# Moving the next image's first score unit out of the MLP's first block to the end of the clustering, with projection fillers kept for behind the group norm

## The chip, the cores and the metric

The kernel runs on one core of a Trainium2 chip. The metric is the device time of one execution in microseconds (us), taken as the median of several runs. All data are 32-bit floats. The engines of a core are called PE (matrix), DVE (vector), ACT (scalar), POOL (GpSimd) and SP (which here only issues DMA transfers).

## The reference

The input is four images of 256 channels and 64 x 64 pixels. Each goes through two layers:

```
# layer 0: self-attention over the 4096 pixels
q = wq x + bq (32 channels);  k = wk x + bk (32);  v = wv x + bv (256)
x = gamma * (v softmax(q^T k)^T) + x
# layer 1
y = x + ls1 * cluster(group_norm(x))     # four-centre clustering in four heads
h = w2 gelu(w1 group_norm(y) + b1) + b2  # 256 -> 1024 -> 256, per pixel
y = y + ls2 * h
z = relu(batch_norm(y * dw_w));  out = relu(batch_norm(pw_w z))
```

Both group norms take one mean and one variance over all channels and pixels of an image.

## The kernel before, in words

The images are worked one after the other, but overlapped. For each image `b` the main loop runs three stages in program order: `weighting` (softmax and weighted sum of the attention, in 8 pixel blocks of 8 units each), `cluster`, and `mlp` (8 blocks of 512 pixels; in the last image but one, 7). The order of instructions on each engine is the order written in the program; a framework adds the semaphores and hands out the buffers.

PE work of the next image is put into the current image's stages in two ways.

- **Fillers.** `parts.projections` is a list of 35 small pieces of the next image's projections: 32 halves of `v` (`v_half`, line 314, four rows of the trace's PE pieces each, and an ACT copy, line 322, after every second one), and, from place 26 on, `k_half(0)` (line 291), `q_four(0)` (line 333, its ACT step is line 341) and `k_half(1)`. `fill(n)` takes the next `n` of the list. They are called wherever PE would wait for another engine: in the weighting's end, in the clustering and in the group norms. `fill(N)` takes all that is left.
- **Score units.** `score(u)` computes a unit of the next image's attention scores: four matmuls (line 363) of 32 rows each, which need the query block in the layout that `q_block` makes with four DMA transfers (line 348). Given the list arguments it copies the two score banks to SBUF with ACT (lines 371 and 372), and appends to the list `maxima` the DVE steps (line 376) that take the running maximum: two of them for unit 0, four for the others. `rest()` takes one step from that list, before and after the third and fourth chunk of each block of the MLP.

In `mlp`, `at` says after which chunk of which block a unit stands. A block has four chunks `j`; each chunk is `first(nb, j)`, seven products of 256 columns (line 1361, tiles hp, hq and hr) and their sums on DVE (line 1352), with the second layer's seven steps (line 1278, tile mo) of the chunk before put between them. `slots` says how many of these seven go to each of four places, and it differs for a chunk that a score unit follows:

```python
                    todo = second_by_seven(nb, acc, hs, j, own, ahead)
                    slots = (0, 2, 2, 3)
                    if scored:
                        slots = (3, 1, 2, 1)
                    elif j == 2 and nb:
                        slots = (3, 1, 0, 3)
```

`norm(nb)` writes the normalised block and its factors, the sums and differences that the seven products need (lines 1239 to 1242). Block 0 has them from DVE, with the scaling (line 1176); later blocks have the factors from POOL, within the third chunk's second-layer steps, which run during the fourth chunk's products.

At the end of the clustering the result is added to the image (`products`, PE line 982, DVE line 994, ACT line 1006 with POOL line 1007), and DVE gathers the second group norm's statistics (line 966). `mlp` then starts with POOL's weight factors (lines 1157, 1158, 1159 and 1162) and `group_norm`: statistics to one mean per partition (DVE, line 243), across partitions (PE, lines 245 and 246, tile gnm), DVE lines 249, 250 and 253, PE line 255 (tile gnv), then the root (DVE 171, ACT 172, DVE 174) and scale and shift (DVE 263 and 264). One filler stands after line 246 and one after the root.

Buffers that matter: the two score banks in PSUM (`ps_s`, two buffers) also serve the products hp, hq and hr and the clustering's `products`; projections use `ps_m` (two); a score's result is one of 14 `spool` tiles; the running maximum is a single buffer.

Of the kernel before, what the change touches and what calls it, by code (L numbers as in the profile page):

```python
# [14 lines left out]
B, C, H, W = 4, 256, 64, 64  # L15
# [3 lines left out]
NBLK = N // NB  # L19
# [26 lines left out]
def attention_then_cluster_block(  # L46
# [17 lines left out]
    nc = tc.nc  # L64
# [22 lines left out]
    def load_x(b, t):  # L87
        xb = x[b].rearrange("(k p) h w -> p k (h w)", p=P)
        xt = spool.tile([P, KC, XT], F32, tag="s", name=f"x_{b}_{t}")
        for k in range(KC):  # L90
            nc.sync.dma_start(out=xt[:, k, :], in_=xb[:, k, t * XT : (t + 1) * XT])
        return xt
# [597 lines left out]

    h64_q = h64[:ED].rearrange("p (q h m) -> p q h m", q=4, h=HEADS)

    def cluster(b, ys, stats, cells, rest, fill, gelu):

        pool = small.tile([P, KC, 4, 4], F32, tag="pool", bufs=1, name=f"pool_{b}")

# [264 lines left out]
        stats2 = small.tile([P, 2 * NBLK, 6], F32, tag="stats", name=f"st2_{b}")  # L961
        pieces = {}

        def seen(hb, c):
            for q in range(4):
                nc.vector.bn_stats(stats2[:, 4 * q + 2 * hb + c, :], pieces[hb, c, q])
# [54 lines left out]
        seen(0, 1)  # L1021
        seen(1, 0)
        seen(1, 1)
        fill(5)
        return stats2


# [104 lines left out]
    def turn_w2(b, kept):  # L1132


        a11, _, a21, a22 = quarters_w2()
        w7 = work.tile([P, h_n, P], F32, tag="rden", bufs=1, name=f"w2_7_{b}")
        nc.gpsimd.tensor_tensor(w7, a21, a11, ALU.subtract)
        s1 = work.tile([P, h_n, P], F32, tag="q", name=f"w2_1_{b}") if kept else a21
        nc.gpsimd.tensor_tensor(s1, a21, a22, ALU.subtract)
        s2 = work.tile([P, h_n, P], F32, tag="q", name=f"w2_2_{b}")  # L1140
        nc.gpsimd.tensor_tensor(s2, s1, a11, ALU.subtract)
        return s1, s2, w7

    def mlp(b, ys, stats2, fill, nxt, blocks, turned):


        W_A, W_CD, W_B, W_D = own_w["q"]
# [101 lines left out]

        for _ in norm(0, nc.vector):  # L1250
            pass
        if nxt:
            nxt.q_block(0, nc.sync)

        def product(out, w, j, x):
            nc.tensor.matmul(out, w[:, j * P : (j + 1) * P], x, start=True, stop=True)
# [179 lines left out]

        hooks, drips, maxima = [], [], []

        def hook():
            while hooks:
# [6 lines left out]
        acc, todo, slots = None, iter(()), (0,) * 4  # L1449
        own = ahead = iter(())  # L1450

        at = {(u, 3): u for u in range(7)} | {(7, 2): 7}
        if blocks < NBLK:
            at |= {(6, 1): 6, (6, 2): 7}
            del at[6, 3]
        for nb in range(blocks):
            end = nb == blocks - 1
            for j in range(4):
# [37 lines left out]
                if scored:  # L1496
                    copies = []
# [37 lines left out]
    def filler(todo):  # L1535
        def fill(n):
            for _ in range(min(n, len(todo))):
                todo.pop(0)()

        return fill  # L1540

    with tc.manual_schedule():
        here = attention(0, xs0)
        here.alone()
        late = None
        for b in range(B):
            xs1, begun = [], []
            nxt = attention(b + 1, xs1) if b + 1 < B else None

            def ahead():  # L1550
                if nxt and len(xs1) < N // XT:
                    xs1.append(load_x(b + 1, len(xs1)))
                elif late and not begun:
                    begun.append(begin())

            begin, todo, gelu = late or (None, list(nxt.projections) if nxt else [], lambda i: None)
            fill = filler(todo)
            stats, cells, rest = here.weighting(ahead, fill, (lambda: None) if b else derived)
            turned = turn_w2(b, not nxt)
            stats2 = cluster(b, here.xs, stats, cells, rest, fill, gelu)  # L1560

            late = mlp(b, here.xs, stats2, fill, nxt, NBLK - (b == B - 2), turned)
            here = nxt


# [74 lines left out]
```

## Time and profile before

| what | us |
|---|---|
| median of 3 runs (lowest to highest) | 3378.88 (3378.66 to 3379.28) |
| the profiled execution's own time | 3378.26 |
| its span, first to last instruction | 3376.5 |
| PE busy | 3318.5 |
| DVE busy | 2226.3 |
| POOL busy | 1929.7 |
| ACT busy | 1687.1 |

The busy times of different engines overlap, so they don't add up to the span. A row of the timeline gives the start, the duration of a run of equal instructions, the engine, the line, and in brackets how long the engine had been idle and which engine ended that. PE matmuls overlap with their successors by design; the distance between starts is what one costs.

### The profile page before, as it was taken

Reading aid. Unit: us, or ns where it says so; the run is one execution under the profiler, and the core shown is the slowest. Engines: PE = TensorE matmul, PEld = TensorE weight load, DVE = VectorE, ACT = ScalarE, POOL = GpSimd, SP = SyncE. Lnnn points to the kernel's source line nnn. Section 1 sums busy time; section 2 is a strip of 40 time slices with the busy share of each in tenths; the row PEclk is TensorE's granted clock in tenths of the full one; section 3 lists DMA queues with packets and bytes.
Section 4 is the critical chain, followed back from the end, with each engine's and each line's share of the span. In section 5 each row is a group of like instructions: output and inputs, shape, how many; then the busy total and the mean of one; then the engine's idle time right before and its main releaser. Section 6 shows DMA issues by size and latency. Waiting matters only on the chain.

```text
span 3376.5 us, 34772 instructions
## 1 busy us (share of the span) xinstructions
PE 3318.5 (98%) x12322; PEld 1815.5 (54%) x12322; DVE 2226.3 (66%) x3546; ACT 1687.1 (50%) x2253; POOL 1929.7 (57%) x1366
## 2 busy tenths in 40 slices
PE   8999999999999999999999999999999999999999
PEld 4434445788533444578843334457873344346686
DVE  5667664677666766467766676646766766764675
ACT  5545543445555554345555555434555555544444
POOL 2655666366365666536645566554644676573664
PEclk9999999999999999999999999999999999999999
DMA  2000002000000000100000000020000000010000
GB/s 71 13 13 11 16 7 86 4 13 19 25 13 13 13 13 22 70 4 19 14 29 13 10 13 13 22 71 4 20 26 13 13 13 13 10 39 1 13 20 26
DMA packets 43102, 70.99 MB, mean 21 GB/s; under 512 B 9680, under 2 KB 18480, under 8 KB 42928
## 3 DMA queue, kind: packets, MB, share of 16 engines
q1 hardware_dynamic: 38064, 61.94, 5.5%
q10 hardware_dynamic: 4608, 6.30, 0.8%
q8 instruction: 97, 1.59, 0.2%
q14 instruction: 77, 0.63, 0.1%
q0 software_dynamic: 256, 0.52, 0.1%
HBM read 43.46 MB, written 16.89 MB: 18 GB/s over the span
## 4 chain that ended last, share of the span: by engine, by line
PE 94%; DVE 4%; ACT 1%; POOL 0%; issue 0%; DMA 0%; SPq 0%; ACTq 0%; POOLq 0%; DVEq 0%
PE av L477 53%; PE mo L1278 10%; PE sc L363 8%; PE hq L1361 5%; PE hp L1361 3%; PE hr L1361 3%; PE vp L314 2%; PE fv L861 2%; PE mo L1262 1%; PE hq_pw L1361 1%; PE pw L1215 1%; PE hr_pw L1361 1%; PE op L982 1%; PE hp_pw L1361 1%; PE qp L333 0%; PE kp L291 0%
## 5 line engine op out<-in xcount | busy, mean ns | idle before, releaser
L477 PE MATMUL av<-s,v 128*128 128x512 f32 x4096 | 1819.2, 598 | 0.6 <-ACT s L467 0.6
L472 POOL TENSOR_TENSOR acc<-acc,s 128x1024 f32<-128x1024 f32 x448 | 1057.1, 2360 | 538.3 <-ACT s L467 519.5
L477 PEld LDWEIGHTS av<-s,v 128*128 128x128 f32 x4096 | 759.0, 190 | 1044.8 <-issue 1034.5
L467 ACT ACTIVATE s<-s 128x1024 f32<-128x1024 f32 x512 | 541.0, 1059 | 591.1 <-DVE s L464 550.2
L464 DVE TENSOR_TENSOR s<-s,mb 128x1024 f32<-128x1024 f32 x512 | 595.8, 1206 | 18.4 <-ACT mb L448 16.7
L385 DVE TENSOR_TENSOR top<-sc,top 128x1024 f32<-128x1024 f32 x196 | 239.4, 1222 | 374.7 <-PE sc L363 374.6
L1316 ACT ACTIVATE hs<-hs,pv_s 128x256 f32<-128x256 f32 x496 | 233.3, 505 | 339.2 <-DVE hs L1352 339.2
L1278 PE MATMUL mo<-hs,w 128*128 128x256 f32 x1512 | 387.9, 382 | 0.0
L381 ACT COPY s<-sc 128x1024 f32<-128x1024 f32 x224 | 225.1, 1005 | 225.6 <-PE sc L363 225.6
L1278 PEld LDWEIGHTS mo<-hs,w 128*128 128x128 f32 x1512 | 282.0, 190 | 60.2 <-ACT hs L1316 19.9
L363 PE MATMUL sc<-q,k 32*128 32x512 f32 x2048 | 299.9, 640 | 0.4 <-ACT s L386 0.4
L388 DVE TENSOR_TENSOR top<-sc,top 128x1024 f32<-128x1024 f32 x196 | 240.1, 1225 | 72.6 <-ACT s L381 59.6
L386 ACT COPY s<-sc 128x1024 f32<-128x1024 f32 x224 | 227.3, 1015 | 66.0 <-DVE top L383 36.1
L1352 DVE TENSOR_TENSOR hs<-hq,hs 128x256 f32<-128x256 f32 x496 | 198.5, 421 | 75.5 <-PE hq L1361 65.2
L469 POOL TENSOR_TENSOR acc<-s 128x1024 f32<-128x1024 f32 x32 | 75.3, 2352 | 287.6 <-ACT s L467 287.6
L1285 POOL TENSOR_TENSOR hs<-hs 128x256 f32<-128x256 f32 x108 | 82.3, 762 | 194.5 <-ACT hs L1369 91.4
L363 PEld LDWEIGHTS sc<-q,k 32*128 32x128 f32 x2048 | 86.4, 182 | 183.1 <-issue 122.0
L1352 DVE TENSOR_TENSOR hs<-hp,hs 128x256 f32<-128x256 f32 x124 | 52.1, 420 | 143.0 <-ACT hs L1369 143.0
L1361 PE MATMUL hr<-xn,w 128*128 128x256 f32 x496 | 127.5, 379 | 0.5 <-DVE hs L1352 0.5
L314 PE MATMUL vp<-wv_s,x 128*128 128x256 f32 x512 | 123.4, 387 | 0.2 <-ACT v L322 0.2
L314 PEld LDWEIGHTS vp<-wv_s,x 128*128 128x128 f32 x512 | 93.5, 190 | 25.5 <-issue 10.5
L1361 PEld LDWEIGHTS hr<-xn,w 128*128 128x128 f32 x496 | 94.1, 190 | 19.1 <-issue 4.8
(261 smaller groups left out, 3528.0 us busy)
## 6 DMA issues: line engine op xcount, KB each, us to landing
x<-in_x SPq DMA_DIRECT2D x32, 512.0 KB, 6.7
out<-xn SPq DMA_DIRECT2D x62, 256.0 KB, 2.1
w<-in_w SPq DMA_DIRECT2D x8, 1024.0 KB, 10.7
mr<-row_mx SPq DMA_DIRECT2D x28, 256.0 KB, 3.1
rden<-row_rd SPq DMA_DIRECT2D x28, 256.0 KB, 3.1
q<-q ACTq DMA_DIRECT2D x96, 64.0 KB, 2.0
mix<-in_wfv SPq DMA_DIRECT2D x8, 192.0 KB, 8.4
q<-q SPq DMA_DIRECT2D x24, 64.0 KB, 2.1
```

Source lines behind the costliest of these rows:

```text
L314: nc.tensor.matmul(vps[0][:, i % 2, :], xs[i * P // XT][:, k, o : o + P], wv_s[:, k, :], start=(k == 0), stop=(k == KC - 1),)
L363: nc.tensor.matmul(halves[r // 2][:, r % 2, :], k_s[rows, g, :], q_s[rows, :], start=True, stop=True)
L385: nc.vector.tensor_tensor(top, halves[1], top, ALU.max)
L388: nc.vector.tensor_tensor(top, halves[0], top, ALU.max)
L464: nc.vector.tensor_tensor(sh, sh, mxs[nb].unsqueeze(1).to_broadcast([P, 2, NB]), ALU.subtract)
L467: nc.scalar.activation(sh, sh, AF.Exp)
L472: nc.gpsimd.tensor_tensor(acc, acc, s[:, 2 * h : 2 * h + 2], ALU.add)
L477: nc.tensor.matmul(av[c], own["v"][:, RG * g + quarter, c * P : (c + 1) * P], slots[u][:, quarter, :], start=(g == 0 and quarter == 0), st ...
L1278: return nc.tensor.matmul(bank[:, half * HB : (half + 1) * HB], a[:, j], t, start=start, stop=stop)
L1316: nc.scalar.activation(src, src, AF.Gelu_apprx_tanh, bias=pvc("b1", P, j + 4 * (i > 1)))
L1352: nc.vector.tensor_tensor(dst, ps, term, ALU.add)
L1361: nc.tensor.matmul(out, w, x, start=True, stop=True)
```

## The change

For an image that has a next one, the end of `cluster` no longer takes five fillers. It issues `q_block(0)` of the next image, takes three fillers, and computes score unit 0 with both its copies. The two fillers not taken there remain in the list for `group_norm` and `fill(N)` in `mlp`. In `mlp` the issue of `q_block(0)` and the place of unit 0 after block 0's fourth chunk go away, and with it the slots of a scored chunk there. The list `maxima` is made in the main loop and passed on, so unit 0's two maximum steps are taken in block 0 instead of block 1.

```diff
-    def cluster(b, ys, stats, cells, rest, fill, gelu):
+    def cluster(b, ys, stats, cells, rest, fill, gelu, nxt, maxima):
...
         seen(1, 1)
-        fill(5)
+        if not nxt:
+            fill(5)
+            return stats2
+
+        nxt.q_block(0, nc.sync)
+        fill(3)
+        copies = []
+        nxt.score(0, copies, maxima)
+        copies.pop()()
         return stats2
...
-    def mlp(b, ys, stats2, fill, nxt, blocks, turned):
+    def mlp(b, ys, stats2, fill, nxt, blocks, turned, maxima):
...
         for _ in norm(0, nc.vector):
             pass
-        if nxt:
-            nxt.q_block(0, nc.sync)
...
-        hooks, drips, maxima = [], [], []
+        hooks, drips = [], []
...
-        at = {(u, 3): u for u in range(7)} | {(7, 2): 7}
+        at = {(u, 3): u for u in range(1, 7)} | {(7, 2): 7}
...
-            stats2 = cluster(b, here.xs, stats, cells, rest, fill, gelu)
-
-            late = mlp(b, here.xs, stats2, fill, nxt, NBLK - (b == B - 2), turned)
+            maxima = []
+            stats2 = cluster(b, here.xs, stats, cells, rest, fill, gelu, nxt, maxima)
+
+            late = mlp(b, here.xs, stats2, fill, nxt, NBLK - (b == B - 2), turned, maxima)
```

Line numbers behind the change move by up to 8 in the changed kernel (line 1361 becomes 1367, line 1352 becomes 1358, line 1240 becomes 1248).

## The prediction

> **What bounds the kernel now.** I read three views of the profile, from coarse to fine. First the page: busy times, and the chain that ended last.
>
> ```profile
> PE 3318.5 (98%) x12322; PEld 1815.5 (54%) x12322; DVE 2226.3 (66%) x3546; ACT 1687.1 (50%) x2253; POOL 1929.7 (57%) x1366
> ...
> PE 94%; DVE 4%; ACT 1%; POOL 0%; issue 0%; DMA 0%; SPq 0%; ACTq 0%; POOLq 0%; DVEq 0%
> ```
>
> The matrix engine (PE) is the bound: 3376.5 of span less 3318.5 leaves 58 us of idle in all. A change can win only by putting work into these gaps. So the second view is who PE waited for (us in total, times, longest):
>
> ```profile
> PE hp L1361 <- DVE xn L1240: 4.0, 4, 1.7
> ...
> PE hp L1361 <- DVE hs L1352: 3.6, 4, 0.9
> ...
> PE hp L1361 <- DVE xn L1176: 2.4, 3, 0.8
> ...
> PE gnv_gn L255 <- DVE mv_gn L250: 1.7, 4, 0.4
> ```
>
> These four are in one place, the second group norm and the MLP's first products, once per image; for each of images 0 to 2 the waits in that place are 0.4, 0.8, 0.8 and 0.9 us. The third view is the timeline there, for image 0 (images 1 and 2 repeat it to 0.03 us, 838.52 and 1675.09 us later).
>
> ```profile
> 645.60 2.49 SPq L348 DMA_DIRECT2D q<-q  x4
> ...
> 647.67 3.72 PE L314 MATMUL vp<-wv_s,x 128*128 128x256 f32 x16
> ...
> 650.30 0.59 DVE L243 BATCH_NORM_AGGREGATE mv_gn<-st 128x2 f32<-128x96 f32 x1
> ...
> 651.22 0.28 PE L245 MATMUL gnm_gn<-mv_gn,left 128*128 128x1 f32 x2
> ...
> 651.76 1.27 POOL L1159 TENSOR_TENSOR w_bcd<-w,w_abcd 128x512 f32<-128x512 f32 x1
> 651.96 1.09 DVE L250 SCALAR_TENSOR_TENSOR mv_gn<-dv_gn,mv_gn 128x1 f32<-128x1 f32 x1
> ...
> 653.10 0.38 PE L255 MATMUL gnv_gn<-mv_gn,avg 128*128 128x1 f32 x2 [0.40 <-DVE dv_gn L253]
> ...
> 655.27 0.70 PE L1361 MATMUL hp<-xn,w 128*128 128x256 f32 x2 [0.81 <-DVE xn L1176]
> ...
> 656.74 0.67 PE L1361 MATMUL hp<-xn,w_abcd 128*128 128x256 f32 x2 [0.77 <-DVE xn L1240]
> ```
>
> The reader is to see that a serial VectorE (DVE) chain runs from 650.30 to 656.60 and that PE, with its fillers, is early three times. Every f32 matmul prints as two pieces, so vp x16 is eight matmuls, four projection halves.
>
> The place that loses the score is the seam between block 0 and block 1 of the MLP:
>
> ```profile
> 678.77 0.73 POOL L1240 TENSOR_TENSOR xn<-xn 128x256 f32<-128x256 f32 x1
> 678.85 0.31 PEld L363 LDWEIGHTS sc<-q,k 32*128 32x128 f32 x8 [0.33 <-issue]
> 678.85 1.14 PE L363 MATMUL sc<-q,k 32*128 32x512 f32 x8
> ...
> 679.92 1.56 PE L1278 MATMUL mo<-hs,w 128*128 128x256 f32 x6
> ...
> 681.32 0.59 PE L1361 MATMUL hp<-xn,w 128*128 128x256 f32 x2
> ```
>
> PE has no gap here: the score is paid in full.
>
> **What the Trainium skill says.** "SBUF — State Buffer", section "SBUF: two separate sides": DVE with two SBUF inputs and GpSimd (POOL) share a port pair under an exclusive lock; whoever starts first keeps it for the instruction. The trace agrees: L250 takes 1.09 us on one element per partition beside POOL's L1159 and ends at 653.05, where POOL ends at 653.03; the same line takes 0.22 at its quickest. "TensorE: Matmul & The Clock Gate", "Step-by-step: what each phase is for": weight loads may be pulled ahead, matmuls stay in program order. So the group-norm matmul stands behind whatever is put ahead of it. The trace agrees in what it shows of order.
>
> **The change, part by part** (per image, for images 0 to 2; image 3 has no next image and is untouched).
>
> *The score's price.* From the mo piece at 677.46 to hp at 681.32 are 3.86 us. Six mo matmuls lie in it; fourteen matmuls of a hidden chunk take 6.04 us (hp at 666.67 to hp at 672.71), 0.432 each, so six take 2.60. The score costs 1.26, with the turn to 32-row weights and back.
>
> *The query DMAs (SP).* Their issue moves ahead in the program, but the SP queue is empty there and they wait only for the query (ACT, L341): they already start at 645.60, before PE is at the fillers. Each takes 0.6 to issue and 2.0 to land, the last at about 649.5. Order on SP is unchanged: no cost. In image 2 one issue took 1.4, and the last lands some 0.8 later.
>
> *PE at the end of the clustering.* After the third k/q projection, two projection halves instead of four: 647.67 plus 4 x 0.432 = 649.40. The score starts at 649.55 (q just landed) and frees PE at 650.62 (1.07 from its first piece to the next instruction). The mean's input is ready at 650.89, so gnm starts at 650.94 instead of 651.01 (its weight load then). The score fits ahead of the chain; had it not, L249 on DVE and all behind it would wait. Its two PSUM banks were last read by DVE's L994, done at 643.15.
>
> *The two fillers moved behind.* After gnm (0.71) one half, 0.86, done at 652.5; gnv is set by L250, and L250 by POOL's L1159, so it stays at 653.10. One half after it, to 654.2; the two left over (fill(N)) to 655.95, where hp (ready at 655.22) now starts, 0.7 late; its partner waits for L1240 until 656.74 as before, and hp needs 0.43. Nothing moves: the score and the halves sit in the 0.40 + 0.81 + 0.77 of idle. Front: 0. Bounds: 0.16 gained (were L250 quicker, L264 would run into POOL's L1162, which ends at 654.25; L264 starts at 654.41), 0.4 lost (a landing of 3.3, the longest on SP, ends the score at 651.9, past the 651.5 from which gnv slips).
>
> *ACT.* The two score copies (1.01 and 1.02) go to about 650.8 to 652.8, where ACT was idle 1.70 ahead of the square root at 653.71. The last projection copy (0.59) goes behind the table load and its probe, 656.6 to 657.2, ahead of the hp copy at 657.45. PE waits for the score copies before hp; both are long done. Cost 0.
>
> *The two maxima (DVE, L376)* move from block 1 to block 0's third chunk. Free they take 0.68 each; DVE is idle 0.95 ahead of 668.19 and 1.86 ahead of 674.24, and POOL's factors for block 1 start only at 677.97. Cost 0. Removed from block 1 they free 1.21 and 0.92 of DVE, contended; a wait for DVE at the pointwise step (hr at 700.57, cold, 0.2 in all) may go: I take 0.15, bounds 0 and 0.2.
>
> *The seam without the score.* It also changes the slots of seven second-layer steps, from (3,1,2,1) to (0,2,2,3). PE reaches hp of block 1 at 677.46 + 1.30 = 678.76, ends it at 679.19, and must wait for POOL's L1240, done at 679.50. With 0.05 to be seen and up to 0.1 for a cold weight load, thirteen matmuls follow (5.62): hp of the next chunk at 685.2 to 685.3, where it was 686.07. Gain 0.85 (1.26 less 0.4). Later POOL steps (L1241 at 680.30, L1242 at 680.99) are ahead of PE. DVE's L1308 now stands ahead of the last two sums of the chunk (0.74): they end at 685.6, their gelu at 686.35, and PE wants it at about 686.5. Bounds: 1.26 (no wait) and -0.5 (rival 1).
>
> Sum per image 0 + 0.85 + 0.15 = 1.0; three images 3.0. Against the profiled execution: span 3376.5 to 3373.5, its time 3378.26 to 3375.3. That execution stands 0.6 below the median shown, so the forecast is 3378.88 - 3.0 = 3375.9. The measurement of this kernel tells about 0.2%, 6.8 us, from no change; 3.0 is 0.09%.
>
> **Rivals.** *1, slower: the seam turns into a POOL wait.* The score was cover for POOL's factors (L1239 to L1242, 0.8 apart). If DVE's two moved maxima land among them, each holds the shared port 0.68, L1240 ends at 680.86, and PE waits 1.7 in place of 1.26: slower by 0.5 per image, 3380.4. It decides from L1240 at about 680.3. For it: in block 1 such pairs slow each other now (L376 1.21, POOL L1239 1.03). Against: by program order the maxima are due 4 us earlier, in idle time.
>
> *2, the landing.* If q lands as late as the longest seen, in all three images, gnm slips and 0.4 of each 1.0 goes: 3377.1. Above 6.5 us of landing it would be slower; nothing shows such a one.
>
> *3, the chain shortens too.* PE leaves L250 room before POOL's L1159, and the seam does not wait: 1.26 + 0.2 + 0.16 = 1.6 per image, 3374.0. Against: L250 would have to come 0.2 earlier than at 651.96, and gnm gains 0.07.
>
> *4, it does nothing:* the seam wait equals the score, 3378.9.
>
> **How the numbers follow.** Forecast 0.50; rival 1 0.10, 2 0.08, 3 0.09, 4 0.08. All these cases lie within 0.2%. The other 0.15 is what I have not listed, first of all the 2.4 us of PE idle per image in the later blocks (busy 177.55 of the 180 us from 710 to 890), which may shift with the seam. I split it into 0.08 for faster by more than 0.2%, 0.07 for slower. The range 3372.8 to 3379.4 takes in rivals 2, 3 and 4, and a further 0.4 per image of later blocks on the fast side; rival 1 stays outside.
>
> **What would show it.** Right: in the profile after, a score (L363) at about 649.6, gnm near 650.95, L250 still about 1.1, hp's second product at 656.7, a new wait of hp for POOL's L1240 of some 0.3 at 679, and the next chunk's hp near 685.2. Wrong: hp's second product moved by over 0.3, PE's waits for POOL at the seam above 1 us, or a time outside the range.

## The result, and the profile after

| | before | after |
|---|---|---|
| median of 22 runs each on the same chip, us | 3378.62 | 3373.27 |
| lowest to highest | 3377.51 to 3379.28 | 3371.66 to 3373.92 |
| profiled execution's own time | 3378.26 | 3372.78 |
| its span | 3376.5 | 3371.0 |

The change saves 5.35 us, a ratio of 0.9984 (95% interval 0.9978 to 0.9990). The forecast was 3375.9, a saving of 3.0. The slowest of the runs after (3373.92) is faster than the fastest before (3377.51). The sign of the change and the places of the predicted gain are right; nearly half of the measured gain is not in the prediction's sum. The rest of this document says where each part lies.

In the changed kernel the lines have moved: what the prediction calls L1361 (the seven products) is L1367, L1352 is L1358, L1278 is L1284, the factors L1239 to L1242 are L1247 to L1250, the scaling L1176 is L1184, and POOL's weights L1159 and L1162 are L1167 and L1170.

The page after, busy times and the engines of the chain that ended last:

```profile
PE 3315.7 (98%) x12322; PEld 1813.0 (54%) x12322; DVE 2226.0 (66%) x3546; ACT 1684.0 (50%) x2253; POOL 1931.1 (57%) x1366
...
PE 93%; DVE 5%; ACT 1%; POOL 1%; issue 0%; DMA 0%; SPq 0%; ACTq 0%; POOLq 0%; DVEq 0%
```

PE is still the bound with the same 12322 pieces. Its busy time fell by 2.8 us although it does the same work. That is worth a stop: moving work does not by itself make it shorter, so it is a hint that some of the same instructions ran faster.

Who PE waited for (us in total, times, longest):

```profile
PE cnt L912 <- DVE scr L831: 9.8, 4, 2.7
...
PE hp L1367 <- DVE hs L1358: 3.6, 4, 0.9
...
PE gnv_gn L255 <- DVE dv_gn L253: 1.9, 4, 0.5
PE hp L1367 <- DVE xn L1248: 1.6, 1, 1.6
...
PE hp L1367 <- POOL xn L1248: 0.8, 4, 0.2
```

The three waits for the scaling (L1176 before) are gone, and those for L1240, 4.0 in four, have come down to a single one of 1.6, in the last image, which the change leaves alone. The gaps are filled. The last row holds the wait that the prediction announced at the seam, once in each of images 0 to 2; the fourth was there before (0.2, once). The first row hardly changed. Before, it read

```profile
PE cnt L912 <- DVE scr L831: 9.9, 4, 2.7
```

It becomes important below.

The timeline of the group norm in image 0. This execution stands 0.52 later than the one before already ahead of the place (the second product, 656.74 before, is at 657.25), so 0.52 is taken off every start when it is compared with the prediction; below this is called "on before's clock".

```profile
646.11 2.49 SPq L348 DMA_DIRECT2D q<-q  x4
...
650.10 1.14 PE L363 MATMUL sc<-q,k 32*128 32x512 f32 x8
...
651.55 0.35 PE L245 MATMUL gnm_gn<-mv_gn,left 128*128 128x1 f32 x2 [0.31 <-DVE mv_gn L243]
...
652.28 1.27 POOL L1167 TENSOR_TENSOR w_bcd<-w,w_abcd 128x512 f32<-128x512 f32 x1
652.36 1.20 DVE L250 SCALAR_TENSOR_TENSOR mv_gn<-dv_gn,mv_gn 128x1 f32<-128x1 f32 x1
...
653.86 2.84 PE L314 MATMUL vp<-wv_s,x 128*128 128x256 f32 x12
...
657.25 0.67 PE L1367 MATMUL hp<-xn,w_abcd 128*128 128x256 f32 x2
```

The reader is to see the score in front of the mean, the three projection halves in one run behind gnv, and the second product where it was. The seam between blocks 0 and 1:

```profile
677.97 1.46 PE L1284 MATMUL mo<-hs,w 128*128 128x256 f32 x6
...
679.26 0.59 PE L1367 MATMUL hp<-xn,w 128*128 128x256 f32 x2
679.29 0.72 POOL L1248 TENSOR_TENSOR xn<-xn 128x256 f32<-128x256 f32 x1
...
680.07 0.70 PE L1367 MATMUL hp<-xn,w_abcd 128*128 128x256 f32 x2 [0.21 <-POOL xn L1248]
...
685.78 0.59 PE L1367 MATMUL hp<-xn,w 128*128 128x256 f32 x2
```

The score is gone, hp comes at once, and its partner starts just after POOL's L1248 ends (680.01): 0.81 behind hp, where 0.43 is the usual distance.

To see where the time went I paired every PE matmul of the two traces and followed the distance between their starts. Per image 0 to 2 it changes by 0.00 across the group norm, by -0.80 across the seam and by -0.17 at the pointwise step of block 1 (hr): -0.99, -0.97 and -0.98. **That is 2.94 us, the forecast's 3.0.** Between the medians 2.4 is left over. In this pair of executions two places that the change does not touch give 1.5 each: the clustering stages of images 1 and 2, at L912 and L891 (the counts and sums of the clusters). The 0.52 of the program's beginning goes the other way. Image 2, before and then after:

```profile
2300.32 1.62 PE L912 MATMUL cnt<-scr,ones 128*96 128x64 f32 x16 [2.71 <-DVE scr L831]
2301.87 2.79 PE L891 MATMUL agg<-vf,sim 128*32 128x96 f32 x64
```

```profile
2297.39 1.57 PE L912 MATMUL cnt<-scr,ones 128*96 128x64 f32 x16 [2.70 <-DVE scr L831]
2298.90 1.53 PE L891 MATMUL agg<-vf,sim 128*32 128x96 f32 x64
```

The same 64 pieces take 2.79 before and 1.53 after, behind the same wait. Busy time by stretch over this stage, images 1 and 2, first the kernel before and then after. The columns are the stretch, its length, busy time of PE, PEld, DVE, ACT and POOL, and then PEclk, the clock that PE was granted:

```profile
core 0: us, PE busy (x) PEld busy (x) DVE busy (x) ACT busy (x) POOL busy (x), PEclk, DMA share, GB/s
1457.00:1473.00 16.00, 13.27 (x120) 10.34 (x119) 5.53 (x15) 6.93 (x13) 0.00 (x0) 0.79 0.01 1
2293.00:2309.00 16.00, 13.27 (x129) 10.55 (x127) 6.62 (x18) 7.12 (x13) 0.00 (x0) 0.89 0.01 1
```

```profile
1457.00:1473.00 16.00, 13.27 (x127) 9.94 (x127) 7.06 (x17) 7.72 (x15) 1.16 (x1) 0.89 0.00 1
2293.00:2309.00 16.00, 13.27 (x132) 9.29 (x131) 8.82 (x19) 8.81 (x16) 2.69 (x3) 1.00 0.00 1
```

PE is as busy, but its clock is higher. In the trace's clock records PE runs at full or at half clock. A half-clock spell lasts 3.41 or 6.83 us; 3.41 is called a unit here. Before, the clustering of image 0 has one unit (at 625.77), image 1 two (at 1462.03) and image 2 one (at 2301.71); after, image 0 has one (626.91), image 1 one (1463.18) and image 2 none. This is what the last column shows: over 16 us one unit gives 1 - 0.5 x 3.41 / 16 = 0.89, two give 0.79. A unit can lengthen PE's own work by at most half of 3.41, 1.7 us; 1.5 was measured for each of the two that went. The Trainium skill, "TensorE: Matmul & The Clock Gate", section "What's actually happening", describes this: an idle and a busy clock state, half clock after at least one idle window of about 3.4 us, and a window that runs freely and does not start anew with the kernel. The traces agree on full and half clock, on 3.41, and on a grid that lies differently in each execution. They differ on what counts as idle: here a wait of 2.70 can be enough.

So two explanations are to be told apart: the remaining 2.4 us are this clock in the clustering, or they are something steady of the order that the pairing shows in the wrong place.

### The profile page after: what moved, and what is told of

Read it like the earlier page. It is cut to its first block, busy times and chain, and to the rows that moved or that the text cites. A ratio compares the mean times of both kernels' runs of the same rounds, so it can differ in the third digit from the quotient of the medians.

```text
span 3371.0 us, 34775 instructions
## 1 busy us (share of the span) xinstructions
PE 3315.7 (98%) x12322; PEld 1813.0 (54%) x12322; DVE 2226.0 (66%) x3546; ACT 1684.0 (50%) x2253; POOL 1931.1 (57%) x1366
## 4 chain that ended last, share of the span: by engine, by line
PE 93%; DVE 5%; ACT 1%; POOL 1%; issue 0%; DMA 0%; SPq 0%; ACTq 0%; POOLq 0%; DVEq 0%
PE av L477 53%; PE mo L1284 9%; PE sc L363 8%; PE hq L1367 5%; PE hp L1367 3%; PE hr L1367 3%; PE vp L314 2%; PE fv L861 2%; PE mo L1268 1%; PE hq_pw L1367 1%; PE pw L1223 1%; PE hr_pw L1367 1%; DVE st L966 1%; PE op L982 1%; PE hp_pw L1367 1%; DVE top L376 0%
## 5 line engine op out<-in xcount | busy, mean ns | idle before, releaser
L1284 PE MATMUL mo<-hs,w 128*128 128x256 f32 x1512 | 387.0, 382 | 0.0
L1284 PEld LDWEIGHTS mo<-hs,w 128*128 128x128 f32 x1512 | 282.5, 190 | 57.7 <-ACT hs L1322 19.8
L1358 DVE TENSOR_TENSOR hs<-hq,hs 128x256 f32<-128x256 f32 x496 | 198.7, 421 | 80.1 <-PE hq L1367 70.1
L1358 DVE TENSOR_TENSOR hs<-hp,hs 128x256 f32<-128x256 f32 x124 | 52.2, 421 | 134.1 <-ACT hs L1375 134.1
L1367 PE MATMUL hr<-xn,w 128*128 128x256 f32 x496 | 127.5, 379 | 0.5 <-DVE hs L1358 0.5
L1367 PEld LDWEIGHTS hr<-xn,w 128*128 128x128 f32 x496 | 94.1, 190 | 19.1 <-issue 4.8
```

The lines of the kernel that those rows point to most:

```text
L1284: return nc.tensor.matmul(bank[:, half * HB : (half + 1) * HB], a[:, j], t, start=start, stop=stop)
L1358: nc.vector.tensor_tensor(dst, ps, term, ALU.add)
L1367: nc.tensor.matmul(out, w, x, start=True, stop=True)
```

## The experiments

Twelve kernels were run in three sets of four, with the kernel before on the same chip in each set. The texts on record name their theories by letters. In the first set A is that the filled gap at the group norm keeps PE's clock up later, B that the distance from image to image, against the clock's window, decides how many spells the clustering pays, and C that it is chance. In the second and third set C is that the rest is the clock in the clustering, O that it is order alone.

| kernel | median, us (runs) | less before of its set | ratio, 95% interval |
|---|---|---|---|
| after (the result) | 3373.27 (22) | -5.35 | 0.9984, 0.9978 to 0.9990 |
| after, again | 3372.68 (21) | -5.90 | 0.9983, 0.9977 to 0.9990 |
| before, fillers moved, score not | 3378.22 (13) | -0.36 | 1.0001, 0.9993 to 1.0009 |
| after, pad of 2 | 3377.32 (13) | -1.26 | 0.9997, 0.9988 to 1.0005 |
| before, group norm covered | 3378.22 (13) | -0.36 | 1.0000, 0.9992 to 1.0008 |
| before, counts covered | 3371.24 (20) | -6.80 | 0.9981, 0.9974 to 0.9988 |
| after, counts covered | 3368.29 (6) | -9.75 | 0.9971, 0.9960 to 0.9982 |
| after, seam slots | 3370.93 (14) | -7.11 | 0.9981, 0.9973 to 0.9989 |
| after, five fillers in front | 3379.47 (13) | +1.43 | 1.0004, 0.9996 to 1.0012 |
| after, counts covered and seam slots | 3367.96 (5) | -9.92 | 0.9969, 0.9956 to 0.9981 |
| after, counts covered, again | 3368.42 (7) | -9.46 | 0.9973, 0.9962 to 0.9984 |
| after, counts covered, pad of 2 | 3371.21 (18) | -6.67 | 0.9979, 0.9972 to 0.9986 |
| after, pad of 8 | 3383.07 (21) | +5.19 | 1.0015, 1.0009 to 1.0022 |

The intervals, 2 to 4 us to each side, are wider than several of the differences below; what follows rests on medians together with the traces. The third column is called the offset below. A trace shows one execution only, and two executions of one kernel can differ by a unit of half clock; so what a trace shows of the clock is checked against the medians.

**After, unchanged, on another occasion.**

> The changed kernel once more, with a second profile. By the order of the work (each image: 0 in front, 0.8 at the seam, 0.2 in block 1, as the first two traces show by matching each PE matmul) it should gain 2.9 us; 5.3 were measured. The 2.4 left over lie where PE runs at half clock for spells of 3.41 us: nine such spells in the profile of before, seven in that of after. Theory A (the filled group-norm gap keeps the clock up) expects few spells here again and 3373.2. Theory B (the places where PE is nearly idle for some 3 us fall differently on the clock's own grid of 3.41 us because images now follow each other 1 us sooner) expects the same time, but spells that differ with the phase of the grid. Theory C (the first profiles were two chance phases, and the 2.4 is no steady effect) expects about 3375.6.

Measured: 3372.68, 5.90 below before. The 5.35 was no chance, so 2.4 to 3.0 are to be explained beside the order. The profiled execution took 3374.51, the slowest of its set and 1.73 more than the first profile of after. It has one unit in image 2's clustering, where the first has none (1.6 more by the pairing), and none in image 3's, where the first has one (1.5 less); most of the 1.73 comes from other places of the half-clock spells around image 3's last group norm. So the clock also moves time about in image 3, which the change leaves alone.

**The fillers alone**: kernel before, three fillers instead of five at the end of the clustering, the score left in block 0.

```diff
-        fill(5)
+        fill(3 if held else 5)
```

> The kernel before with only the hold-back: three fillers instead of five at the end of the clustering, the score left in block 0. Forecast's theory: PE waits some 1.5 us ahead of gnm and less behind it, the chain from L250 stays, and the time is that of before within 0.3 us. Rival: without the score in front the gap ahead of gnm costs, up to 1.7 us per image, 3383. If theory A of the clock holds, PE's idle time in this stretch is the same sum as before, so no gain either.

Measured: 3378.22, no difference from before. Four of its 13 runs took 3380.5 to 3381.0; the profile is of one of these and has a half-clock spell of 6.83 us in the group norm itself, where the clock over the stretch is 0.74:

```profile
651.00:664.00 13.00, 11.59 (x40) 9.15 (x40) 7.49 (x20) 4.87 (x10) 2.86 (x3) 0.74 0.00 0
```

Moving fillers without the score makes a gap (1.38 of idle ahead of the mean) and brings nothing. The gain needs the score's move.

**A pad**: kernel after, one product of block 3's second chunk done three times in images 0 to 2, 6 matmuls of 0.43 in all.

```diff
+            if n in pads:
+                for _ in range(2):
+                    product(p, w_p, e)
```

> The changed kernel with one product of block 3, chunk 1, done three times instead of once (same result), in images 0 to 2: 2 x 0.432 us of PE more per image, 2.6 in all, so that images follow each other almost as far apart as in the kernel before, while the group-norm gap stays filled. Theory A: 3373.2 + 2.6 = 3375.8. Theory B: the spells come back with the old spacing, and the time is about 3378.2, almost that of before. Theory C: 3375.8 or more, with no relation to spells.

Measured: 4.1 to 4.6 above after (by the two values of after). The pairing shows that the pad itself costs 0.73 per image, 2.2 in all, less than the 2.6 of its matmuls; it hides a little waiting. In the clustering the profile has two units in image 1 and one in image 2, as before has, though none in image 0; the pad, half an image away, made the clustering of images 1 and 2 slower. That speaks for B.

**Covering the group norm**: kernel before, four constant products of 256 columns in its group norm's idle time.

```diff
+        if cover:
+            for k in range(4):
+                nc.tensor.matmul(ps1[:, C:], avg, wv_s[:, k % KC, :], start=True, stop=True)
```

> The kernel before with four matmuls of constants (256 columns each, 1.73 us, results unused) put behind the filler that follows the root in the second group norm of images 0 to 2, so that PE's gap ahead of hp is filled as the change fills it, but no work is moved. The order of work gains nothing: hp starts 0.7 later and its partner at the same time. Theory A: 2.4 us faster than before, 3376.1. Theories B and C: 3378.5, as before.

Measured: 3378.22, unchanged. By the pairing the cover costs nothing (the second hp product stays where it was), so it hides no gain. Its one profile has a unit less than before's in image 1, but the median shows no gain of 2.4. A busier group norm does not keep the clock up in the clustering 800 us on. A falls.

**Covering the counts**, in both kernels: constant products in PE's wait ahead of the counts. This takes away what makes the spells and leaves the order alone.

```diff
         ohs = oh.rearrange("p (q j s) -> p q j s", q=4, j=8)
+        for k in range(5 if b < B - 1 else 3):
+            nc.tensor.matmul(cnt_p[:, C:], avg, wv_s[:, k % KC, :], start=True, stop=True)
```

> The kernel before, with constant 256-column products put into PE's wait ahead of the counts (L912): five in images 0 to 2 (5 x 0.43 = 2.15 us in a wait of 2.70), three in image 3 (1.29 in 1.74). The work of the kernel is unchanged, nothing is made later by order. Theory C (clock): the half-clock spells of 3.41 us that follow this wait go, at 1.71 us each; the profile of before has them at 625.8 (one), 1462.0 (two), 2301.7 (one), 3114.1 (one), so it falls by some 7 to 8.5, to about 3370 to 3371.5. Theory O (order alone, the clock plays no part in the difference): it falls by as much as the kernel after does with the same cover, and the difference of the two stays at 5.4 to 5.9. Rival: the spells come from something else (the short matmuls with few rows), and the time stays 3378.6.

> The kernel after with the same cover in the wait ahead of the counts. What it tells is its difference to the kernel before with that cover, on the same chip. Theory C: with the spells of the clustering gone from both, only the order of work is left, 2.9 us; after falls less than before, by 3.5 to 6, to about 3367 to 3368.5. Theory O: the difference stays 5.4 to 5.9, so 3364 to 3366. Rival (spells have nothing to do with the wait): 3372.7, unchanged.

> After with the cover once more, for a closer median (the first time had six runs, 3366.8 to 3370.2). Theory C: 2.9 below before with the cover (3371.2), 3367.8 to 3369. Theory O: 5.4 to 5.9 below it, 3365.3 to 3365.8.

Measured: before falls by 6.80, after by 3.6 to 4.4, to 3368.29 and 3368.42. **The difference of the two is 2.95 in one set, and 2.66 between the offsets of two sets, where it was 5.35 to 5.90: what is left is the order's 2.9.** Before with the cover, the timeline of image 1 and then the stretches of images 0 to 2:

```profile
1459.11 2.32 PE L912 MATMUL cnt<-wv_s,avg 128*128 128x256 f32 x10
1461.97 1.57 PE L914 MATMUL cnt<-scr,ones 128*96 128x64 f32 x16 [0.55 <-DVE scr L831]
1463.47 1.53 PE L891 MATMUL agg<-vf,sim 128*32 128x96 f32 x64
```

```profile
621.00:634.00 13.00, 12.43 (x130) 9.46 (x129) 5.56 (x15) 6.85 (x12) 0.00 (x0) 1.00 0.01 1
1454.00:1470.00 16.00, 15.22 (x150) 11.81 (x150) 8.17 (x21) 7.46 (x14) 0.00 (x0) 1.00 0.01 2
2289.00:2305.00 16.00, 15.22 (x150) 11.81 (x150) 8.17 (x21) 7.46 (x14) 0.00 (x0) 1.00 0.00 1
```

Ten more PE pieces per image make the program shorter: with 0.55 of idle in place of 2.7 the clock is 1.00 in all three images (of after with the cover too), and the sums take 1.53. None of the 15 clustering stages of images 0 to 2 in the five traces with the cover has a half-clock spell; without it 22 of 27 have one. Pairing the matmuls of the two covered kernels gives -0.97, to within 0.04, across the group norm and the MLP of each of images 0 to 2, and no step in the clustering. O falls.

**The pad again, on after with the cover.**

> After with the cover, and with the product of block 3's chunk 1 done three times in images 0 to 2, as in the padded kernel without a cover: 6 matmuls of 0.43, 2.6 by order. There the pad cost 4.6 against after. Theory C (the other 2.0 were spells of the clustering, which the cover takes away): 2.6 above after with the cover, 3370.4 to 3371.4. Rival (the pad's own place costs 4.6): 3372.5 to 3373.

Measured: 2.8 to 3.1 above after with the cover, where without it the same pad cost 4.1 to 4.6; 2.2 of either is the pad itself by the pairing. The pad's own place is not what made it dear. Its profile is of the slowest of its 18 runs, and shows something else: in image 1 one of the four query transfers took 3.9 us to land, PE waited for it in the middle of the score, and the mean came 1.3 late; two units of half clock followed in the group norm. By the pairing with after with the cover this place cost 4.0.

**A pad of one window**: the same product done nine times, eight more matmuls of 0.43 per image; no cover. By the pairing they cost 3.3 per image, 9.9 in all.

> After, without a cover, with that product done nine times in images 0 to 2: 24 more matmuls, 3.45 us per image, which is one period of the clock's grid (3.41), 10.3 in all. Theory B (what the clustering pays depends on where the images stand against the grid): a whole period changes nothing of that, so 10.3 above after, 3382.5 to 3383.7. Rival (any added time pays 1.8 times its length, as two repeats did, or a lump of 2.0): 3385 and more. A further one (the pad hides waits of the blocks behind it): below 3382.

Measured: 3383.07. That is 9.8 above the first value of after, and 10.5 to 11.1 when each is taken against before of its own set. Its profile has one unit in image 0, one in image 1 and none in image 2, as after has. A shift by about one window thus costs its own length and at most 1.2 more, while a shift by about a quarter of one cost 1.9 to 2.4 more. That is what B says.

**All five fillers in front**: kernel after, with `fill(5)` in place of `fill(3)` ahead of the score.

> The kernel after with all five fillers (2.15 us, where three take 1.29) kept at the end of the clustering ahead of the score: only the score is moved, the fillers are not. PE then reaches the group norm's mean 0.86 late, at about 652.3, and the second step of the group norm on DVE (L250) falls among POOL's weights. If the reading is right that the fillers make the room for the score, the front loses 0.9 to 1.3 per image and the seam keeps its gain of 0.8: 0.1 to 0.5 slower per image than before, so by order some 6.5 above after at most, 3376 to 3380. Rival: the front has slack for both (DVE's chain is set elsewhere), and it stays within 0.3 per image of after, 3372.7 to 3373.6.

```profile
653.33 0.38 PE L245 MATMUL gnm_gn<-mv_gn,left 128*128 128x1 f32 x2
...
653.94 1.26 POOL L1170 TENSOR_TENSOR w<-w,w 128x512 f32<-128x512 f32 x1
...
654.17 1.05 DVE L250 SCALAR_TENSOR_TENSOR mv_gn<-dv_gn,mv_gn 128x1 f32<-128x1 f32 x1
```

Measured: 3379.47, 6.8 to 7.3 above after by the offsets. This execution stands 0.92 later than before's ahead of the place. PE reaches the mean at 652.4 on before's clock, and L250 ends with the next of POOL's weights. The front loses 1.2 per image, the seam and block 1 give back 0.97, together 0.2 per image, 0.7 in all, worse than before. Most of the rest to after is the clock: 0.79 in image 2's clustering, 3.1 by the pairing with the first profile of after. So the room that the two moved fillers make is what lets the score in.

**The seam**: kernel after, one second-layer step more ahead of block 1's first product.

```diff
                     slots = (0, 2, 2, 3)
+                    if nxt and (nb, j) == (0, 3):
+                        slots = (1, 1, 2, 3)
```

> The kernel after with the slots of the seven second-layer steps of block 0's last chunk changed from (0,2,2,3) to (1,1,2,3): one such step (0.43) goes ahead of hp's first product, and so covers PE's wait for POOL's xn at the seam. By order 0.2 to 0.4 us per image, 0.6 to 1.2 in all: 3371.5 to 3372.1. A rival: the step is ready too late for its new place (its sum on DVE or gelu on ACT comes behind), and PE waits as long for that: 3372.7. The clock may add or take one or two spells of 1.7 either way (3370 to 3376).

```profile
677.85 1.89 PE L1284 MATMUL mo<-hs,w 128*128 128x256 f32 x8
679.58 0.59 PE L1367 MATMUL hp<-xn,w 128*128 128x256 f32 x2
680.01 0.64 PE L1367 MATMUL hp<-xn,w_abcd 128*128 128x256 f32 x2
```

Measured: 3370.93, 1.2 to 1.8 below after by the offsets; the pairing gives 0.43 per image, 1.3. The two hp products now follow each other by 0.43, and PE no longer waits for POOL between them: the seam wait cost the 0.4 that the prediction took from the score's price.

**Cover and seam together.**

> The kernel after with both: the cover in the wait ahead of the counts, and the slots (1,1,2,3) in block 0's last chunk. If the two gains are independent, the cover's 4.4 to 5 and the seam's 0.4 per image (1.2) add up: 3366.5 to 3367.5. Rival: the seam kernel's gain of 1.7 to 2.3 against after was partly clock, which the cover takes away: then only the order is left, 0.6 to 1.2 below after with the cover, 3367.1 to 3367.7. If the seam gained nothing by order: 3368.3.

Measured: 3367.96 (five runs), 0.2 to 0.5 below after with the cover by the offsets; so few runs do not tell 0.4 from 1.2. The pairing with after with the cover shows the same 0.43 in each of images 0 to 2, 1.3 by order. It is the lowest median of all, 9.92 below before. Most of it is the cover.

## Why the prediction was right, and what it lacked

- **The score's price, 1.26.** Right: without the score the second hp product is at 680.07, 679.55 on before's clock, and the first at 678.74 where 678.76 was worked out. With the wait gone too, in the seam kernel, 0.80 + 0.43 = 1.23 of the 1.26 are won.
- **The seam's wait, 0.4.** Right: POOL's L1248 ends at 679.49 on before's clock (679.50 was worked out); hp of the next chunk starts at 685.26, inside 685.2 to 685.3. Net -0.80 by the pairing, -0.85 in the sum. The seam kernel shows the wait by taking it away. Rival 4, the wait as long as the score, is thereby out.
- **Rival 1, the maxima among POOL's factors.** It did not come: the two L376 of image 0 ran at 667.67 and 672.80, 0.68 each, in idle time as argued. The 0.15 for block 1 was measured as 0.17.
- **The front, 0.** Right: score at 649.58 (649.55 was worked out), the mean's weight load at 651.00 (650.94), L250 still held to the end of L1167 (1.20), gnv at 653.10, second product at 656.73, all on before's clock. It was closer than the prediction thought: L250 came at 651.84, 0.12 earlier than before, and only 0.08 behind the start of POOL's L1167. Five fillers in front give the loss of 1.2 that lay behind "the score fits ahead of the chain". Rival 3 needed a free L250 and no wait at the seam, and neither came; that its 3374.0 lies near the measured 3373.27 is chance.
- **The landing.** Rival 2 did not come in the profile after: the transfers start at 645.59 on before's clock, where they did, and in image 2 the score is drawn out to 1.52 us from 1.14 and the mean still comes in time. It is real, though: it came once in the 30 group norms of the ten profiles with the score at its new place, in that of after with the cover and the pad of 2, with a landing of 3.9 us, longer than the 3.3 of which the prediction knew.
- **The range held in part by luck.** Its fast side, 3372.8, was rival 3 with 0.4 more per image from the MLP's later blocks. Neither came, and the clock, which is not in it, filled the place. The second measurement, 3372.68, lies just below it.
- **The step that failed is the sum's silence on the clock.** The prediction took the same instruction to cost the same wherever the image stands in time, and put "what I have not listed" (0.15) at the later blocks of the MLP. Those stayed as they were to 0.1 us. What was not listed is the clustering: PE waits 2.7 us there for DVE, and none, one or two units of half clock follow, at about 1.5 each. The waits of before show it (cnt L912), and its stretches show a clock of 0.79 and 0.89; a reader of the page's chain alone sees nothing of it. It was worth 2.4 to 3.0, as much as the whole forecast.

Why does a shift of 1 us per image make fewer spells, and not only other ones? The kept traces show the link. Take where the counts (L912) begin behind the last mark of the clock's grid (laid through the starts of the trace's half-clock spells, every 3.4133 us), as a share of this window, and the units of half clock in that clustering stage:

| kernel | image 0 | image 1 | image 2 |
|---|---|---|---|
| before | 0.83: 1 | 0.07: 2 | 0.59: 1 |
| before, fillers moved | 0.39: 0 | 1.00: 2 | 0.55: 1 |
| before, group norm covered | 0.49: 1 | 0.74: 1 | 0.85: 1 |
| after, five fillers in front | 0.55: 1 | 0.85: 1 | 0.02: 2 |
| after, pad of 2 | 0.33: 0 | 0.03: 2 | 0.51: 1 |
| after | 0.66: 1 | 0.60: 1 | 0.40: 0 |
| after, again | 0.73: 1 | 0.69: 1 | 0.51: 1 |
| after, seam slots | 0.78: 1 | 0.61: 1 | 0.29: 0 |
| after, pad of 8 | 0.69: 1 | 0.61: 1 | 0.38: 0 |

In all 27 stages the place decides: none from 0.29 to 0.40, one from 0.49 to 0.85, two from 1.00 on to 0.07. And a unit delays the next image by 1.5, so the images hang together. Before, images 0 and 1 follow each other, with one unit between them, at 837.07 us, 0.23 of a window over 245 windows: from "one" the next image drifts up, towards "two". After, they follow at 836.05 and 835.60, 0.06 and 0.20 under 245: from "one" it drifts down, towards "none". The pad of 8 adds about a whole window and goes with after; the five fillers in front are spaced like before and go with it.

What stays open is the size. The places were read from one execution of each kernel; no kernel was made to set them, and the average saving was not worked out from them. Nor do the profiles show why a unit costs 1.5 and not 1.7. From the profile of before alone the prediction could not have had the number of units, since the grid lies differently in each execution.

## What to carry to other kernels

When a sum over moved work is right by order and the time still differs, look at the granted clock in the stages that the change did not touch: here a shift in time alone changed it. Where PE waits some 2.7 us once per image, constant products in the wait can be worth more than reordering: here 6.8 us in one place, against 2.9 for the reordering. And when a fixed piece of work leaves a place where it covered a wait, what is gained is its price less the next wait; here the timeline before gave both to about 0.05.

## What the runs showed of the hardware

- Half-clock spells are 3.41 or 6.83 us long, but for the one at each program's end, and within one execution they start on one grid: before, image 1's starts at 1462.03 and image 2's at 2301.71, 839.68 apart, which is 246 x 3.4133. From one execution to the next the grid lies differently.
- A wait of 2.70 us can be enough for a spell: in images 0 to 2 of nine traces 22 of 27 such waits had one, and the place of the wait's end on the grid told which. A wait of 0.55 was not enough in any of 15.
- Busy time alone does not show a lowered clock. In image 2's clustering PE was busy for 13.27 of 16 us before and after, at a clock of 0.89 and of 1.00, while the same 64 pieces of the sums took 2.79 us and 1.53.
